# The last four tiles' output projection in another order, the last tile finished in quarters, and new durations for the planner: an attention and mixture kernel on one core

## The chip, the core and the metric

One NeuronCore of a Trainium2 chip runs the whole kernel. Its engines work side by side: TensorE (PE in the profile; PEld is its weight load), VectorE (DVE), ScalarE (ACT), GpSimd (POOL), and the queue SP, which issues the DMAs. The metric is the time of one execution on the device, in microseconds (us).

## What is computed

The input is four sequences of 512 tokens with 1024 features, in float32.

```python
x = x + layernorm(attention(layernorm(x)))   # 32 heads of 32, 8 key/value heads, rotary, causal
x = x + layernorm(ffn(layernorm(x)))
# ffn(x): the logits of 8 experts; the two largest, by softmax, weigh the experts' low-rank products
result = x @ base_w.T + base_b
low = einsum('bsd,erd->ebsr', x, lora_A)                        # rank 16
result += 2.0 * einsum('ebsr,eor,bse->bso', low, lora_B, w_full)
```

Each layernorm has no learned factors: it subtracts the mean and divides by the root of the variance and 1e-5.

## The kernel before

**Tiles.** The 2048 tokens are 16 tiles of 128. They are worked through in the order 0 to 11, 13, 14, 15, 12, in pairs (`pairs`, L834): the last two pairs are (13, 14) and (15, 12). Tile 12 is the first of its sequence and so attends to 128 keys alone; tile 15 attends to 512.

**Stages of a tile.** x is normalised (`normed_x`, L871) and transposed (pt_xn); keys and values come from a weight that stays on chip (acc_kv); q comes from streamed weights (acc_q), is rotated on DVE and POOL (`rotate`, L744) and transposed (pt_q; pt_k for keys). Scores (sc, `scores`, L1364) go to PSUM; DVE adds the mask and takes the maximum (nmax, L1451), ACT the exponentials (pr, L1393), POOL multiplies by the inverse sum (L1407), PE transposes (pt_p, L1467), ACT or DVE copies (prT), and PE multiplies by the values (av, L1490), which are copied to aT. The output projection o (acc_o) goes with its bias to the tile w; two layernorms follow (`attended`, L1050): w normalised is added to y, which holds x, and y normalised goes back to w. w is transposed (pt_h) and copied (T_h); the gates and the low-rank product (acc_gl, pt_low) and the base weight f (acc_f, with one matmul of the lora weight in each sum) follow, and a last layernorm, whose result is added to y and written out (`finished`, L1246). All plain matmuls have one line, that of `project` (L602).

**Products of pairs.** For a pair of tiles q, o and f are each made by seven products of half size rather than eight (`seven`, L641), from sums of the tiles' halves (s_q, s_o, s_f) and of the weights' quarters ("mixed", written to DRAM at the start). The last pair (15, 12) goes tile by tile (`whole`, L620): two accumulations of eight matmuls of 512 columns, nine for f.

**What orders the work.** The instructions are recorded by a planner in the kernel itself (`Order`, L92). It holds a clock for PE and one for each other engine. Each operation is written with a duration in us and an urgency, and is issued on the engine that can begin it first; each PE step names what it needs. `tensor` (L236) takes the next PE step from several lanes: scores, transposes, values, and three lanes of plain matmuls: the gates' (gl), the keys' (kv), and the main one, with q, o and f in the order that the kernel's last lines write down. A lane whose first step is not ready by the planner's clock is passed over. So the durations do nothing on the chip: they decide only the order in which each engine's instructions stand. PE's own costs are among them: `TILING` (L32) is added for a step of small tiled matmuls (scores, values), `PAIRED` (L33) where a score step and a value step go together. `LANDS` (L376) is the time from a DMA's issue to its data.

**Weights.** Pieces of 128x512 (256 KB) come in the order of the main lane through a ring of 13 buffers (`bring_pieces`, L476), on SP's queue, which also loads x and y and writes the output.

**The end.** Before, the main lane ends with f of (13, 14), o of 15, o of 12, f of 15, f of 12. The last tile's `finished` takes statistics of each half (L511), the mean and variance (L519), the root on POOL (L527), the shift (L531), then w = w*rstd + shift for each half on DVE or ACT (L546, L552), y + w on POOL or DVE (L343), and the DMA of each half (L1264).

Of the kernel before, what the change touches and what calls it, by code (L numbers as in the profile page):

```python
# [11 lines left out]
F32 = mybir.dt.float32  # L12
AF = mybir.ActivationFunctionType
ALU = mybir.AluOpType
AX = mybir.AxisListType

P = 128
# [11 lines left out]

SIGNAL = 0.1  # L30
FILL = 0.3
TILING = 0.4  # L32
PAIRED = 0.55  # L33
TURNING = 0.05
SAFE = 0.3

# [229 lines left out]
def kernel(  # L266
# [72 lines left out]
    def combine(urgent, out, in0, in1, op, engines=("dve", "pool")):  # L339


        def issue(engine):
            engine.tensor_tensor(out=out(), in0=in0(), in1=in1(), op=op)  # L343

        on = {"dve": (0.68, partial(issue, nc.vector)), "pool": (1.3, partial(issue, nc.gpsimd))}
        return Op(urgent, **{e: on[e] for e in engines})


# [24 lines left out]
    wlora_sb = const.tile([P, D], F32, name="wlora_sb")  # L373
    bbase_sb = const.tile([P, D], F32, name="bbase_sb")

    LANDS = 2.0  # L376
    RATE = 370.0
    loaded = {}

# [115 lines left out]
    class Norm:  # L495


        def __init__(self, name, urgent):
            self.name, self.urgent = name, urgent
            self.stats = None  # L500

        def half(self, src, h):
# [11 lines left out]
        def scale(self):  # L514
            name = self.name

            def aggr():
                self.mv = small.tile([P, 2], F32, tag="mv", bufs=4, name=f"mv_{name}")
                nc.vector.bn_aggr(out=self.mv, in_=self.stats)  # L519

            def eps():
                self.veps = small.tile([P, 1], F32, tag="veps", bufs=4, name=f"veps_{name}")
                nc.vector.tensor_scalar_add(self.veps, self.mv[:, 1:2], EPS)  # L523

            def root():
                self.rstd = small.tile([P, 1], F32, tag="rstd", bufs=4, name=f"rstd_{name}")
                nc.gpsimd.tensor_tensor(out=self.rstd, in0=self.veps, in1=neg_half, op=ALU.pow)  # L527

            def shift():
                self.shift = small.tile([P, 1], F32, tag="shift", bufs=4, name=f"shift_{name}")  # L530
                nc.gpsimd.tensor_scalar(  # L531
                    self.shift, self.mv[:, 0:1], self.rstd, -1.0, ALU.mult, ALU.mult
                )

            yield dve(0.2, self.urgent, aggr)
            yield dve(0.15, self.urgent, eps)
            yield pool(0.6, 0, root)
            yield pool(0.4, 0, shift)

        def apply(self, dst, src, h):  # L540
            cols = slice(h * 512, (h + 1) * 512)
            yield Op(
                self.urgent,
                dve=(
                    0.7,
                    lambda: nc.vector.tensor_scalar(  # L546
                        dst()[:, cols], src()[:, cols], self.rstd, self.shift, ALU.mult, ALU.add
                    ),
                ),
                act=(  # L550
                    0.65,
                    lambda: nc.scalar.activation(  # L552
                        dst()[:, cols], src()[:, cols], AF.Identity, bias=self.shift, scale=self.rstd
                    ),
                ),
            )
# [35 lines left out]
    def project(lhsT, w, n, name, needs, take):  # L592


        acc = []
        steps = []

        def issue(c):
            if not acc:
                acc.append(ps.tile([P, 512], F32, tag="ps", name=f"acc_{name}"))  # L600
            last = c == len(needs) - 1
            nc.tensor.matmul(  # L602
                acc[0][:, :n], lhsT=lhsT(c), rhs=w(c), start=(c == 0), stop=last
            )
            if last:
                start(take(acc[0], steps_of[c].done), order.now)

        for c in range(len(needs)):
            us = 0.858 if n == 512 else 0.24
            steps.append(Step(us, partial(issue, c), needs[c], bank=(c == 0)))  # L610
        steps_of = list(steps)
        return steps
# [4 lines left out]
            start(piece.used(step.done))  # L617
        return steps

    def whole(name, tok_name, k, lhsT, ready, take, room, used=None, more=None):  # L620
# [6 lines left out]
        return with_pieces(  # L627
            used,
            project(
                lambda c: lhsT()[:, c, :] if c < ND else more[0](),  # L630
                lambda c: used[c].sb if c < ND else more[1],
                512,
                f"{name}_{tok_name}_{k}",
                needs,
                take,
            ),
        )
# [106 lines left out]
    def rotate(raw, n, i, name):  # L744

        nh, half = n // HD, HD // 2
        yield turn_slots.take()
        turn = ropes.tile([P, 512], F32, tag="turn", name=f"turn_{name}")
        raw3, turn3 = (a[:, :n].rearrange("p (h d) -> p h d", d=HD) for a in (raw, turn))
        for a, b in ((0, half), (half, 0)):  # L750
            sin = rope_sb[:, i, 1, a : a + half].unsqueeze(1).to_broadcast([P, nh, half])
            yield dve(
                0.1 + n * 0.00065,
                2,
                lambda: nc.vector.tensor_tensor(
                    out=turn3[:, :, a : a + half],
                    in0=raw3[:, :, b : b + half],
                    in1=sin,
                    op=ALU.mult,
                ),  # L760
            )
# [6 lines left out]
        yield dve(  # L768
            0.1 + n * 0.0012,
            2,  # L770
            lambda: nc.vector.tensor_add(raw[:, :n], raw[:, :n], turn[:, :n]),
        )
        turn_slots.give(order.at)
# [472 lines left out]
    def finished(tok):  # L1246

        t = tok.t
        norm = Norm(f"4_{t}", 3)
        halves = [Task() for _ in range(NH)]  # L1250
        added, out_halves = [Task() for _ in range(NH)], [Task() for _ in range(NH)]

        def ended(h):
            yield from norm.half(lambda: tok.w, h)
            halves[h].finish(order.at)

        def out_half(h):
            yield from norm.apply(lambda: tok.w, lambda: tok.w, h)
            yield from add_half(lambda: tok.y, lambda: tok.w, h, 2, tok.last)
            added[h].finish(order.at)  # L1260
            cols = slice(h * 512, (h + 1) * 512)
            yield sp(
                0.7,
                lambda: nc.sync.dma_start(  # L1264
                    out=out[t * P : (t + 1) * P, cols], in_=tok.y[:, cols]
                ),
            )
            yield LANDS
            out_halves[h].finish(order.at)

        def rest():
# [10 lines left out]
        return ended  # L1282

    def ffn(pair):

# [43 lines left out]
        def take(h, acc, done):  # L1329
# [34 lines left out]
    def scores(g):  # L1364
# [19 lines left out]
        def quadrant(r):  # L1384
# [264 lines left out]
    order.tensor(score_lane, turn_lanes, value_lane, [gl_lane, kv_lane, main_lane])  # L1649
# [77 lines left out]
```

## Time and profile before

| What | us |
|---|---|
| median of the runs (three, 1186.48 to 1186.75) | 1186.6 |
| the profiled execution's own time | 1187.5 |
| its span, from the first to the last instruction | 1185.7 |
| TensorE busy in it | 1145.5 |
| VectorE busy | 823.9 |
| GpSimd busy | 608.0 |
| ScalarE busy | 533.1 |
| share of the DMA engines' time that the hardware queue took | 59.0% |

The page of the profile gives each engine's busy time and cuts the span into 40 slices of 29.6 us; a digit is a slice's busy share in tenths. PEclk is the granted clock of TensorE, also in tenths. A row of the timeline has the start, the length, the engine, the line, the operation, what it writes and reads, and in brackets the idle time of its engine just before it with what ended that. An x at a row's end counts instructions; a float32 matmul of 512 columns is two of them, 0.43 us each.

### The profile page before, as it was taken

How to read it: one execution, taken by the hardware profiler on the slowest of the kernel's cores; microseconds unless marked ns; L12 is line 12 of the kernel's file. 1: busy time of each engine (PE TensorE's matmuls, PEld its weight loads, DVE VectorE, ACT ScalarE, POOL GpSimd, SP SyncE). 2: the span in 40 equal slices, each digit the busy share in tenths (PEclk: the TensorE clock that was granted, in tenths of full speed). 3: DMA queues.
4: the chain of work that ended last, by engine and by line, in shares of the span. 5: the costliest groups of instructions: out<-in, count | busy, mean ns of one | idle time of the engine just before them, and what ended most of it. 6: DMA issues, size and time to landing. Idle time of an engine off the chain costs nothing.

```text
span 1185.7 us, 21412 instructions
## 1 busy us (share of the span) xinstructions
PE 1145.5 (97%) x7248; PEld 627.0 (53%) x7248; DVE 823.9 (69%) x1609; ACT 533.1 (45%) x1555; POOL 608.0 (51%) x857
## 2 busy tenths in 40 slices
PE   7999999999999999999999999999999999998996
PEld 3445545555556555565545555556655555545443
DVE  4687877875778756787667775678866786675353
ACT  0355544555555345454524334456543554552010
POOL 2575866553656536456455444545544564544221
PEclk9999999999999999999999999999999999998998
DMA  9869768434672636635377344762457645573883
GB/s 347 292 233 350 248 216 264 152 124 152 218 253 74 195 119 226 206 108 174 120 244 244 126 160 143 226 210 81 161 179 244 214 134 164 168 267 110 284 303 110
DMA packets 118315, 232.52 MB, mean 196 GB/s; under 512 B 13504, under 2 KB 14528, under 8 KB 118208
## 3 DMA queue, kind: packets, MB, share of 16 engines
q1 hardware_dynamic: 118208, 231.16, 59.0%
q8 instruction: 58, 0.95, 0.3%
q14 instruction: 49, 0.40, 0.1%
HBM read 210.14 MB, written 20.97 MB: 195 GB/s over the span
## 4 chain that ended last, share of the span: by engine, by line
PE 80%; DVE 8%; DMA 4%; POOL 4%; ACT 2%; issue 1%; SPq 0%; POOLq 0%; ACTq 0%; DVEq 0%
PE acc_f L602 19%; PE acc_o L602 15%; PE acc_q L602 11%; PE pt_p L1467 11%; PE acc_kv L602 7%; PE sc L1372 6%; PE av L1490 6%; PE acc_gl L602 2%; DVE nmax L1451 2%; POOL pr L1407 2%; ACT pr L1393 1%; PE pt_h L577 1%; DVE sc L1441 1%; DMA mix_o<-in_w_o_dram 1%; PE pt_q L996 1%
## 5 line engine op out<-in xcount | busy, mean ns | idle before, releaser
L1407 POOL TENSOR_SCALAR pr<-pr,rtot 128x256 f32<-128x256 f32 (+3 forms) x512 | 303.9, 610 | 249.3 <-DVE rtot L1422 183.9
L1393 ACT ACTIVATE pr<-sc,nmax 128x256 f32<-128x256 f32 (+3 forms) x512 | 264.6, 537 | 108.7 <-DVE nmax L1451 60.8
L1451 DVE TENSOR_REDUCE nmax<-sc 128x2 f32<-128x768 f32 (+3 forms) x176 | 198.2, 1126 | 32.6 <-ACT pr L1393 28.7
L1467 PE MATMUL pt_p<-ident,pr 128*128 128x128 f32 x1280 | 174.2, 276 | 3.5 <-POOL pr L1407 1.6
L1467 PEld LDWEIGHTS pt_p<-ident,pr 128*128 128x128 f32 x1280 | 144.1, 141 | 61.4 <-issue 46.5
L335 ACT COPY prT<-pt_p 128x512 f32<-128x512 f32 (+1 forms) x264 | 135.2, 548 | 83.6 <-PE pt_p L1467 82.9
L1441 DVE TENSOR_TENSOR sc<-sc,cmask 128x256 f32<-128x256 f32 (+2 forms) x176 | 96.7, 549 | 41.0 <-PE sc L1372 35.0
L602 PE MATMUL acc_kv<-wkv_sb,T_xn 128*128 128x512 f32 x256 | 119.4, 600 | 0.0
L335 ACT COPY aT<-av 128x128 f32<-128x128 f32 (+2 forms) x82 | 25.6, 312 | 195.0 <-PE av L1490 195.0
L1393 ACT ACTIVATION_READ_ACCUMULATOR pr<-sc,nmax 128x1 f32 x512 | 108.9, 213 | 0.0
L602 PE MATMUL acc_f<-piece,T_h 128*128 128x512 f32 x232 | 108.7, 596 | 0.0
L602 PE MATMUL acc_o<-piece,aT 128*128 128x512 f32 x232 | 106.3, 595 | 0.5 <-DMA piece<-in_w_o_dram 0.3
L602 PE MATMUL acc_q<-piece,s_q 128*128 128x512 f32 x224 | 105.1, 597 | 1.2 <-DVE raw_q L713 0.9
L602 PE MATMUL acc_o<-piece,s_o 128*128 128x512 f32 x224 | 103.4, 593 | 0.7 <-PE av L1490 0.7
L602 PE MATMUL acc_f<-piece,s_f 128*128 128x512 f32 x224 | 103.6, 593 | 0.0
L602 PE MATMUL acc_q<-piece,T_xn 128*128 128x512 f32 x224 | 102.7, 594 | 0.0
L343 POOL TENSOR_TENSOR y<-y,w 128x512 f32<-128x512 f32 x62 | 80.1, 1307 | 29.5 <-ACT w L552 15.1
L1372 PE MATMUL sc<-kT,qT 32*128 32x384 f32 (+3 forms) x1024 | 93.9, 464 | 0.6 <-ACT pr L1393 0.6
L527 POOL TENSOR_TENSOR rstd<-veps,neg_half 128x1 f32<-128x1 f32 x64 | 35.2, 554 | 114.5 <-DVE veps L523 114.2
L1490 PEld LDWEIGHTS av<-prT,v 128*32 128x32 f32 x2560 | 64.5, 109 | 49.8 <-issue 39.3
L1490 PE MATMUL av<-prT,v 128*32 128x128 f32 x2560 | 88.1, 276 | 0.0
L336 DVE COPY prT<-pt_p 128x512 f32<-128x512 f32 (+1 forms) x88 | 56.2, 641 | 32.2 <-PE pt_p L1467 31.5
(151 smaller groups left out, 1406.5 us busy)
## 6 DMA issues: line engine op xcount, KB each, us to landing
piece<-in_w_o_dram SPq DMA_DIRECT2D x116, 256.0 KB, 3.8
piece<-in_w_base_dram SPq DMA_DIRECT2D x116, 256.0 KB, 3.3
piece<-mixed_q SPq DMA_DIRECT2D x112, 256.0 KB, 3.5
piece<-mixed_o SPq DMA_DIRECT2D x112, 256.0 KB, 4.3
piece<-mixed_f SPq DMA_DIRECT2D x112, 256.0 KB, 3.4
piece<-in_w_qkv_dram SPq DMA_DIRECT2D x100, 256.0 KB, 3.7
xa<-in_x_dram SPq DMA_DIRECT2D x32, 256.0 KB, 4.1
y<-in_x_dram SPq DMA_DIRECT2D x16, 512.0 KB, 5.3
```

Of the source, the lines that this page charges most:

```text
L335: act=(0.15 + n * 0.00085, lambda: nc.scalar.copy(out(), in_())),
L336: dve=(0.15 + n * 0.00105, lambda: nc.vector.tensor_copy(out(), in_())),
L343: engine.tensor_tensor(out=out(), in0=in0(), in1=in1(), op=op)
L527: nc.gpsimd.tensor_tensor(out=self.rstd, in0=self.veps, in1=neg_half, op=ALU.pow)
L602: nc.tensor.matmul(acc[0][:, :n], lhsT=lhsT(c), rhs=w(c), start=(c == 0), stop=last)
L1372: nc.tensor.matmul(sc[:, r, c * n : (c + 1) * n], lhsT=tok.qT[g.kt][rows, (g.at + c) % GROUP, :], rhs=seq.kT[g.kt][rows, :n], start=True, ...
L1393: lambda: nc.scalar.activation(pr[:, c * n : (c + 1) * n], sc4[:, r, c, :], AF.Exp, bias=nmax[:, r, c : c + 1], accum_out=total[:, r, c : ...
L1407: lambda: nc.gpsimd.tensor_scalar(pr[:, c * n : (c + 1) * n], pr[:, c * n : (c + 1) * n], rtot[:, r, c : c + 1], 1.0, ALU.mult, ALU.mult,),
L1441: lambda: nc.vector.tensor_tensor(out=diag, in0=diag, in1=cmask.unsqueeze(1).unsqueeze(1).to_broadcast([P, q, g.n, P]), op=ALU.add,),
L1451: lambda: nc.vector.tensor_reduce(nmax[:, some, : g.n], sc4[:, some], AX.X, ALU.max, negate=True),
L1467: nc.tensor.transpose(pt[:, j, :], g.pr[r][:, j * P : (j + 1) * P], ident)
L1490: nc.tensor.matmul(av[r * HD : (r + 1) * HD, c, :], lhsT=g.seq.v[j][:, head * HD : (head + 1) * HD], rhs=g.prT[r][:, c * (i + 1) + j, :], ...
```

## The change

It has four parts.

1. The durations that the planner works with are set to others: TILING and PAIRED are lower, the two-input operations on DVE, the layernorm's step on ACT, the rotation, the exponentials and LANDS are longer, the layernorm's step on DVE is shorter.
2. In the main lane, the first half of o of tile 15 now stands ahead of f of (13, 14), the second half behind it.
3. f of the last tile (12) is made in four accumulations of 256 columns; each weight piece is used by two of them, and sum, bias and statistics follow each.
4. The end of the last tile: as soon as the root is there, DVE computes y = w*rstd + y for each half, and ACT adds the shift, which POOL makes meanwhile.

```diff
-TILING = 0.4
-PAIRED = 0.55
+TILING = 0.3
+PAIRED = 0.46
...
-        on = {"dve": (0.68, partial(issue, nc.vector)), "pool": (1.3, partial(issue, nc.gpsimd))}
+        on = {"dve": (0.85, partial(issue, nc.vector)), "pool": (1.3, partial(issue, nc.gpsimd))}
...
-    LANDS = 2.0
+    LANDS = 2.8
...
+        def quarter(self, src, k):
...
+            yield dve(
+                0.4,
+                self.urgent,
+                lambda: nc.vector.bn_stats(out=self.stats[:, k, :], in_=src()[:, cols]),
+            )
...
             yield pool(0.6, 0, root)
+            if rooted:
+                rooted.finish(order.at)
             yield pool(0.4, 0, shift)
...
                 dve=(
-                    0.7,
+                    0.66,
...
                 act=(
-                    0.65,
+                    0.82,
...
-            us = 0.858 if n == 512 else 0.24
+            us = {512: 0.858, 256: 0.432}.get(n, 0.24)
...
-                0.1 + n * 0.00065,
+                0.1 + n * 0.00088,
...
-            0.1 + n * 0.0012,
+            0.1 + n * 0.0013,
...
         def out_half(h):
-            yield from norm.apply(lambda: tok.w, lambda: tok.w, h)
-            yield from add_half(lambda: tok.y, lambda: tok.w, h, 2, tok.last)
+            cols = slice(h * 512, (h + 1) * 512)
+            y = tok.y[:, cols]
+            if tok.last:
+                yield dve(
+                    0.75,
+                    0,
+                    lambda: nc.vector.scalar_tensor_tensor(
+                        y, tok.w[:, cols], norm.rstd, y, ALU.mult, ALU.add
+                    ),
+                )
+                yield shifted
+                yield act(
+                    0.65,
+                    0,
+                    lambda: nc.scalar.activation(y, y, AF.Identity, bias=norm.shift),
+                )
+            else:
+                yield from norm.apply(lambda: tok.w, lambda: tok.w, h)
+                yield from add_half(lambda: tok.y, lambda: tok.w, h, 2)
...
         def rest():
-            yield halves
-            yield from norm.scale()
+            yield quarters if tok.last else halves
+            start(scaled(), order.at)
+            yield rooted if tok.last else shifted
...
+        def take_quarter(k, acc, done):
+            yield done
+            cols = slice(k * 256, (k + 1) * 256)
+            yield dve(
+                0.42,
+                0,
+                lambda: nc.vector.tensor_add(tok.w[:, cols], acc[:, :256], bbase_sb[:, cols]),
+            )
+            banks.give(order.at)
+            yield from ended[0](k)
...
-                    0.42 + n * 0.00092,
+                    0.5 + n * 0.00079,
...
-                    0.3 + n * 0.00085,
+                    0.33 + n * 0.00089,
...
-    for n, pair in enumerate(pairs[:-1]):
+    for n, pair in enumerate(pairs[:-2]):
         out_of(pair)
         if n + 2 < len(pairs):
             q_of(pairs[n + 2])
         ffn_of(pair)
-    for tok in pairs[-1]:
-        out_of([tok])
+
+    out_of(pairs[-2])
+    late, behind = pairs[-1]
+    at = len(main_lane)
+    out_of([late])
+    first_half, second_half = main_lane[at : at + ND], main_lane[at + ND :]
+    del main_lane[at:]
+    main_lane.extend(first_half)
+    ffn_of(pairs[-2])
+    main_lane.extend(second_half)
+    out_of([behind])
     for tok in pairs[-1]:
         ffn_of([tok])
```

`ND` is 8, the number of matmuls of one half of o; `late` is tile 15 and `behind` tile 12.

More of the change, by code (lines that the diff above doesn't have):

```diff
@@ L500, in __init__ @@
             self.stats = None
+        def quarter(self, src, k):
+            if self.stats is None:
+                self.stats = small.tile(
+                    [P, 2 * NH, 6], F32, tag="stats4", bufs=1, name=f"stats_{self.name}"
+                )
[5 more added lines that the diff above has]
+            )
         def half(self, src, h):
@@ L512, in half, with scale @@
             )
-        def scale(self):
+        def scale(self, rooted=None):
             name = self.name
@@ L618, in with_pieces, with whole @@
         return steps
-    def whole(name, tok_name, k, lhsT, ready, take, room, used=None, more=None):
+    def whole(name, tok_name, k, lhsT, ready, take, room, used=None, more=None, cols=None):
         used = used or block(name, plain, 0, k) + block(name, plain, 1, k)
@@ L630, in whole @@
                 lambda c: lhsT()[:, c, :] if c < ND else more[0](),
-                lambda c: used[c].sb if c < ND else more[1],
-                512,
-                f"{name}_{tok_name}_{k}",
+                lambda c: (used[c].sb if c < ND else more[1])[:, cols or slice(0, 512)],
+                cols.stop - cols.start if cols else 512,
+                f"{name}_{tok_name}_{k}" + (f"_{cols.start}" if cols else ""),
                 needs,
@@ L1251, in finished @@
         added, out_halves = [Task() for _ in range(NH)], [Task() for _ in range(NH)]
+        quarters, rooted, shifted = [Task() for _ in range(2 * NH)], Task(), Task()
         def ended(h):
@@ L1255, in ended, with ended_quarter @@
             halves[h].finish(order.at)
+        def ended_quarter(k):
+            yield from norm.quarter(lambda: tok.w, k)
+            quarters[k].finish(order.at)
         def out_half(h):
-            yield from norm.apply(lambda: tok.w, lambda: tok.w, h)
-            yield from add_half(lambda: tok.y, lambda: tok.w, h, 2, tok.last)
+            cols = slice(h * 512, (h + 1) * 512)
[17 more added lines that the diff above has]
+                yield from add_half(lambda: tok.y, lambda: tok.w, h, 2)
             added[h].finish(order.at)
-            cols = slice(h * 512, (h + 1) * 512)
             yield sp(
@@ L1264, in out_half @@
                 lambda: nc.sync.dma_start(
-                    out=out[t * P : (t + 1) * P, cols], in_=tok.y[:, cols]
+                    out=out[t * P : (t + 1) * P, cols], in_=y
                 ),
@@ L1269, in out_half, with scaled @@
             out_halves[h].finish(order.at)
+        def scaled():
+            yield from norm.scale(rooted)
+            shifted.finish(order.at)
         def rest():
-            yield halves
-            yield from norm.scale()
+            yield quarters if tok.last else halves
+            start(scaled(), order.at)
+            yield rooted if tok.last else shifted
             for h in range(NH):
@@ L1281, in finished @@
         start(rest())
-        return ended
+        return ended_quarter if tok.last else ended
     def ffn(pair):
@@ L1336, in take @@
             yield from ended[0](h)
-        steps = []
+        def take_quarter(k, acc, done):
+            yield done
+            cols = slice(k * 256, (k + 1) * 256)
+            yield dve(
+                0.42,
+                0,
+                lambda: nc.vector.tensor_add(tok.w[:, cols], acc[:, :256], bbase_sb[:, cols]),
+            )
+            banks.give(order.at)
+            yield from ended[0](k)
+        steps = []
+        if tok.last:
+            for h in range(NH):
+                used = block("f", plain, 0, h, 2) + block("f", plain, 1, h, 2)
+                for q in range(2):
+                    steps += whole(
+                        "f",
+                        tok.t,
+                        h,
+                        tok.hT_tile,
+                        tok.h_ready,
+                        partial(take_quarter, 2 * h + q),
+                        [],
+                        used,
+                        (lowT(0), (lo, hi)[h], [tok.low_done, loaded["lora"]]),
+                        slice(q * 256, (q + 1) * 256),
+                    )
+            return steps
         for h in range(NH):
```

## The prediction

> **What bounds the kernel.** I read the page's busy times first, then its 40 slices, then the stretches around the two slices that are not full, then TensorE's waits.
>
> ```profile
> PE 1145.5 (97%) x7248; PEld 627.0 (53%) x7248; DVE 823.9 (69%) x1609; ACT 533.1 (45%) x1555; POOL 608.0 (51%) x857
> PE   7999999999999999999999999999999999998996
> PEclk9999999999999999999999999999999999998998
> ```
>
> TensorE (PE) is the bound. The change takes none of its work away, so a gain can only come from PE's idle time and from what follows its last matmul. The idle lies in the first slice, in slice 37 (where the granted clock dips too) and in the last. The stretches, with columns for length, busy time by engine, granted clock and DMA:
>
> ```profile
> 20.00:150.00 130.00, 123.06 (x750) 65.85 (x748) 97.06 (x167) 59.48 (x196) 85.25 (x115) 1.00 0.82 287
> ...
> 1064.70:1070.60 5.90, 0.01 (x1) 0.02 (x1) 3.92 (x13) 5.31 (x30) 3.07 (x8) 0.92 0.20 67
> 1070.60:1077.00 6.40, 6.36 (x24) 4.90 (x25) 3.33 (x7) 1.07 (x2) 6.30 (x14) 0.54 0.00 0
> 1077.00:1131.00 54.00, 53.40 (x186) 25.88 (x184) 24.05 (x58) 6.48 (x11) 15.35 (x20) 1.00 0.73 239
> ```
>
> PE does nothing for 5.90 us, and then works 6.4 us at a clock of 0.54. The timeline says what it waited for:
>
> ```profile
> 59.05 0.63 PE L996 MATMUL pt_q<-ident,raw_q 128*128 128x128 f32 x4 [1.51 <-DVE raw_q L771]
> 107.36 0.63 PE L996 MATMUL pt_q<-ident,raw_q 128*128 128x128 f32 x4 [1.27 <-DVE raw_q L771]
> 224.33 0.63 PE L996 MATMUL pt_q<-ident,raw_q 128*128 128x128 f32 x4 [1.28 <-DVE rank L1163]
> 1070.61 2.23 PE L577 MATMUL pt_h<-ident,w 128*128 128x128 f32 x8 [5.90 <-DVE rtot L1422]
> ```
>
> All idle rows of PE sum to 30.1 us: 7.0 at the start, 5.9 here, 1.2 in small waits after it, and **16.1 in some 25 small waits before 1064**. Of those, 8.4 are transposes of rotated q and k (pt_q, pt_k). The end, from the last matmul's results at 1176.54 to 1185.7, is 9.2:
>
> ```profile
> 1178.49 0.55 POOL L527 TENSOR_TENSOR rstd<-veps,neg_half 128x1 f32<-128x1 f32 x1 [12.79 <-DVE veps L523]
> 1179.14 0.27 POOL L531 TENSOR_SCALAR shift<-mv,rstd 128x1 f32<-128x1 f32 x1
> 1179.44 0.81 ACT L552 ACTIVATE w<-w,shift,rstd 128x512 f32<-128x512 f32 x1 [15.61 <-POOL shift L531]
> 1180.07 1.26 POOL L343 TENSOR_TENSOR y<-y,w 128x512 f32<-128x512 f32 x1 [0.67 <-DVE w L546]
> 1180.29 1.60 DVE L343 TENSOR_TENSOR y<-y,w 128x512 f32<-128x512 f32 x1 [0.30 <-ACT w L552]
> 1181.91 0.81 SPq L1264 DMA_DIRECT2D out_dram<-y  x2
> ```
>
> **Step 1: the first half of o for tile 15 moves into the gap.** I compared the orders of the built programs, which hold no time. In the changed one, eight acc_o matmuls of tile 15 stand between tile 15's last value product and pt_h of tile 13, where there was one of another product. Each is two passes of 0.43, so they fill 6.9 us. Only the last of them waits for the newest copy into aT; their weight pieces are the next of a ring of 13, and the DMA share of 0.20 and 0.00 in the gap shows that the queue had nothing left to do, so no transfer is late.
>
> The wait does not vanish, since VectorE's (DVE) chain gets later: the last product of tiles 13 and 14 now puts two matmuls ahead of the last scores (1.7 us), so on equal work the last maximum (L1451) ends at 1066.2 instead of 1064.4. Behind it on DVE stand four rows of 0.69 (an add, three statistics), 0.55 for w, two aggregates of 0.2, two of 0.15, a reciprocal of 0.2: 4.2 us, and 0.2 for GpSimd's (POOL) add; then two roots of 0.55 and two shifts of 0.27 on POOL, of which DVE waits out 0.9; then 1.0 for tile 14 and 0.55 for tile 13's half: 1073.0. PE ends the eight at 1071.3 (the values at 1064.4 and 6.9). A wait of 1.7 us remains.
>
> The clock: in the window 20 to 150 PE waited up to 1.51 us at a time at a granted clock of 1.00, so a wait of 1.7 should not lower it. From pt_h to the last group's pt_p, PE has 4.5 us of work and took 7.5 at the low clock. The same stretch after the change: pt_h from 1073.0 to 1073.9, T_h copied at 1074.6 (behind an add of 0.69), four gl matmuls (0.93), one f (0.86), four gl, two f: pt_p at 1079.0. Before, it began at 1078.1 with nine matmuls (7.7) less behind it. **Gain 6.9.** Bounds: 0 if the chain ends as much later as work was moved; 8.9 if both the idle 5.9 and the 3.0 at half clock go.
>
> The Trainium skill, "TensorE: Matmul & The Clock Gate", Part 1, says that the clock is halved after an idle window of about 3.4 us and comes back after one as long of work. The trace agrees: 5.90 us idle, then 0.54. By that rule the 1.7 us is harmless, and one twice as long would not be.
>
> **Step 2: the planner's durations.** They change every engine's order, on 73 to 74 score-value pairs and the same number of switches between tiled and plain matmuls, so PE's own work stays equal (the two sums of rows by duration differ by under 0.1). The four narrow last products take 36 rows of 256 columns for 18 of 512: at 0.116 for 136 columns and 0.43 for 512 the price follows the columns, so nothing. What changes is how much PE work stands between a chain's start and its transposes. For tile 0's second half of q (the 1.51) it was six matmuls, four pt_p and two pt_xn, 7.8 us; now 9.1. The others: 9.1 to 9.9 (wait 0.53), 7.3 to 8.2 (1.27), 8.7 to 15.2 (0.94), 17.8 to 28.6 (0.60), 12.6 to 17.8 (0.68), pt_k 4.2 to 7.8 (0.88) and 6.3 to 6.4 (0.70); one falls, 15.4 to 14.2 (1.28). Taking each wait less its added cover leaves 3.7 of 8.4. Against it: the first pt_p of tile 2 has 6.9 us of cover where the smallest that stood without a wait is 8.1 (1.2), and one value product of tile 1 follows its transposes at once, so it waits out a copy of 0.59 and the hand-over (0.9). **Gain 2.6.** The other 7.7 of small waits I leave as they are. Bounds: all 16.1 go; or as much again is lost as I expect to win.
>
> **Step 3: the end.** The last add and statistics are over 256 columns. The add has a row (v, 0.42 against 0.69); the statistics have none: between 0 and 0.69, and I take 0.37, by the add's ratio. Saved 0.6. Then DVE does w*rstd+y twice; no row has it at this size; I take 0.69, the two-input add alone (ends: 0.55 of w, 1.60 of the add beside POOL). It no longer waits for the shift, but starts beside it, and the add of 1.60 above, which ended 0.56 after POOL's, shows that it will first wait: 0.28. So after rstd: 0.09 + 0.28 + 0.69 + 0.69 = 1.75 for the second half, ScalarE's (ACT) add of the shift 0.81 (row L552), hand-overs: 2.76, when its DMA is issued. Before, the last DMA was issued 3.28 after rstd. Saved 0.5, and 0.1 since the two transfers lie apart. **Gain 1.2**, bounds 0.3 to 2.0.
>
> The Trainium skill, "SBUF — State Buffer", Who interferes with whom, says that a DVE instruction with two SBUF inputs and a reading GpSimd instruction exclude each other for a whole instruction. That speaks against step 3; without it the sum would be 0.3 better.
>
> The tile-12 pt_low is now followed at once by the matmul that needs its copy (0.41 wait, the row of tile 15 before), while tile 15's gets half a pt_h between: nothing in sum.
>
> **Sum.** 6.9 + 2.6 + 1.2 = 10.7. The profiled run took 1187.5 (span 1185.7 and 1.8 around it), 0.9 over the median shown: 1176.8 by its own time, **1175.9** by the median.
>
> **Rivals.**
> - Steps 1 and 3 pay, the new order elsewhere nothing, or costs 2: 1178.5 to 1180.5. For: the 7.7 of other waits are reshuffled blindly. Chance 0.22.
> - The small waits fall by 6 to 8: 1170.5 to 1172.5. For: seven of nine covers grew by 0.8 us or more. 0.15.
> - pt_h's chain ends later than worked out (each row of mine can meet POOL, as the 1.60 does), the wait grows to where the clock falls again. That lies between 1.51 us, which left it at 1.00, and 5.90, which did not; at the middle, 3.7, it is 2.0 more idle and 2.4 of slow clock: 1180.3. 0.08.
> - The change does nothing that can be measured (0.2% is about what can be told): 0.04.
> - **Slower.** Longer planned chains put plain matmuls earlier, and the last tiles' attention (960 to 1050) is left without filler: eight groups of tile 15 each waiting for pr. It turns the result from 13.1 us of such waits on (10.7 and 2.4), 1.6 per group: 1190 and above. Against: the cover of those groups is 9.7 to 11.9 us against 8.7 to 13.2 before, and 900 to 1050 is full today. 0.08.
>
> The forecast has 0.43, from 1173 to 1178. Eight in ten: 1170 to 1182. Faster 0.88, same 0.04, slower 0.08.
>
> **What would show it.** Step 1: the row pt_h near 1070 has an idle of 1 to 2.5 us and a granted clock of 1.00 follows. Step 2: the pt_q rows' idle sums to under half. Step 3: from the last matmul's result to the last DMA issue 4.7 us instead of 5.8. Wrong if the 0.54 clock is back, or PE idles over 3 us at a new place.

## The result, and the profile after

The changed kernel takes **1167.5 us** (median of five runs, 1167.1 to 1170.9) against 1186.6 (1185.2 to 1188.0): a ratio of 0.984, with a 95% interval of 0.9822 to 0.9858. It is 19 us faster, nearly twice the 10.7 forecast, and 2.5 below the range's end of 1170. The profiled execution took 1167.07 by its own time, with a span of 1165.3 (before: 1187.52 and 1185.7).

The busy times and the slices of the changed kernel, from its page:

```profile
PE 1139.3 (98%) x7284; PEld 632.8 (54%) x7284; DVE 829.1 (71%) x1635; ACT 529.2 (45%) x1543; POOL 601.5 (52%) x847
PE   7999999999999999999999999999999999999997
PEclk9999999999999999999999999999999999999999
```

Slice 37 is full and its clock is back. The 36 more instructions of PE are the narrow products. What TensorE (PE) still waits for (the dots stand for rows left out): the total, how often, and the longest of each:

```profile
PE pt_xn L593 <- DVE xa L562: 7.3, 1, 7.3
PE pt_q L1013 <- DVE rtot L1496: 1.8, 1, 1.8
PE pt_xn L593 <- DVE prT L336: 1.1, 1, 1.1
PE pt_p L1541 <- DVE raw_k L951: 1.1, 1, 1.1
PE pt_h L593 <- DVE w L562: 0.9, 1, 0.9
PE pt_p L1541 <- DVE prT L336: 0.7, 1, 0.7
...
PE pt_k L962 <- DVE raw_k L788: 0.5, 1, 0.5
```

The sum of PE's idle rows falls from 30.1 to 17.8. The small waits ahead of the gap, 16.0 before in 27 rows (16.1 in the prediction; 8.4 of them for pt_q and pt_k), are 8.4 now (1.8 and 0.5 for pt_q and pt_k).

The stretch of the gap, in PE's timeline:

```profile
1053.89 7.13 PE L618 MATMUL acc_o<-piece,aT 128*128 128x512 f32 x16
1061.97 1.06 PE L593 MATMUL pt_h<-ident,w 128*128 128x128 f32 x8 [0.94 <-DVE w L562]
1063.38 1.19 PE L618 MATMUL acc_gl<-wgl_sb,T_h 128*128 128x136 f32 x8 [0.35 <-DVE T_h L336]
```

and in windows around it (length, busy PE, PEld, DVE, ACT, POOL, granted clock, DMA share, GB/s):

```profile
1060.80:1062.00 1.20, 0.26 (x2) 0.07 (x2) 1.20 (x3) 0.49 (x1) 1.20 (x3) 1.00 0.90 258
1062.00:1068.00 6.00, 5.65 (x31) 3.93 (x32) 4.95 (x15) 0.30 (x1) 5.90 (x13) 1.00 0.46 152
```

The sixteen passes of o fill the place, the wait is 0.94 where it was 5.90, and the clock behind it is 1.00 where it was 0.54.

**Where the 19 us come from.** For each amount of PE work done, the two traces give the time at which PE began the next piece. The difference is the **lead** of the changed kernel. It is 1.9 at 63 us, 5.3 at 118, 6.9 at 174, 9.4 at 255, and stands at 7 to 12 until the gap, where it is 10.6. It is 17.9 behind the gap and 18.7 at the last matmul. So the new durations brought **10.6** (nine of it in the first 250 us), the gap **7.3**, and 0.8 came behind it. The end adds 1.6: from the last matmul's result to the end of the span 7.53, before 9.17.

These four add up to 20.3, where the two profiled executions differ by 20.4; the medians differ by 19.1. A lead comes from one execution of each kernel. Six runs (the changed kernel and five of those below) have one and the same order up to the gap, and their leads at 1040 are 10.6, 10.6, 10.5, 10.2, 9.0 and 8.0. So a difference of up to 2.6 in a lead can be the execution's alone.

### The profile page after: what moved, and what is told of

It is laid out like the page before. It is cut to its first block, busy times and chain, and to the rows that moved or that the text cites. A ratio compares the mean times of both kernels' runs of the same rounds, so it can differ in the third digit from the quotient of the medians.

```text
span 1165.3 us, 21509 instructions
## 1 busy us (share of the span) xinstructions
PE 1139.3 (98%) x7284; PEld 632.8 (54%) x7284; DVE 829.1 (71%) x1635; ACT 529.2 (45%) x1543; POOL 601.5 (52%) x847
## 4 chain that ended last, share of the span: by engine, by line
PE 90%; DVE 5%; ACT 2%; POOL 1%; issue 1%; DMA 1%; POOLq 0%; ACTq 0%; SPq 0%; DVEq 0%
PE acc_f L618 19%; PE acc_o L618 16%; PE acc_q L618 15%; PE pt_p L1541 12%; PE acc_kv L618 9%; PE sc L1446 7%; PE av L1564 6%; PE acc_gl L618 2%; PE pt_q L1013 1%; DVE nmax L1525 1%; PE pt_xn L593 1%; PE pt_h L593 1%; ACT pr L1467 1%; DMA xa<-in_x_dram 1%; DVE sc L1515 1%
## 5 line engine op out<-in xcount | busy, mean ns | idle before, releaser
L618 PE MATMUL acc_f<-piece,T_h 128*128 128x512 f32 (+1 forms) x264 | 108.7, 541 | 0.0
```

The costliest lines, as they stand in the source:

```text
L618: nc.tensor.matmul(acc[0][:, :n], lhsT=lhsT(c), rhs=w(c), start=(c == 0), stop=last)
```

## The experiments

The theory formed after the result (**A**): the 10.6 comes from planned durations that now agree with the trace. The planner holds a start for every PE step, so the plan's starts can be laid beside the trace's. Beside the trace of before, PE is 5.3 us behind its own plan at 80 us, 10.0 at 160 and 11.1 at 242; with the new durations it is never more than 2.4 behind up to 800. The rivals: **B**, the move of o and the end were undersized; **C**, any new set of durations draws a new order, and this was a lucky draw; **D**, the cheaper tiled steps pay; and, later, that more cover pays, however much (cover is the PE work that stands between a chain's start and the PE step that waits for the chain's end). Each run is compared with the kernel before on its own chip; its interval is 95%. 

### Parts alone and parts left out

The changed kernel with all durations as before (three of the lines of part 1 are shown; all of them are set back):

```diff
-TILING = 0.3
+TILING = 0.4
...
-        on = {"dve": (0.85, partial(issue, nc.vector)), "pool": (1.3, partial(issue, nc.gpsimd))}
+        on = {"dve": (0.68, partial(issue, nc.vector)), "pool": (1.3, partial(issue, nc.gpsimd))}
...
-    LANDS = 2.8
+    LANDS = 2.0
```

> The changed kernel with all the planner's old durations; o of tile 15 moved, the quarters and the new end kept. Up to 1040 us its order is that of the kernel before. Theory A (the durations alone make the gain ahead of 1050 us, by giving chains more cover; the lead there was 10.6 us): only the gap at pt_h of tile 13 and the end are won, 7.3 + 1.7, so 1177.6. Theory B (the moved o and the end set off more than I counted, and the durations bring the 2.6 forecast): 1170.

Measured: 1176.2, ratio 0.991 (0.9894 to 0.9925). The lead is 1.1 at 1037 and 10.3 behind the gap.

The kernel before with all the new durations (the same lines the other way round):

> The kernel before with all the new durations and nothing else. Up to 1040 us its order is that of the changed kernel. Theory A: lead of 10.6 us at 1050, the idle of about 5 us at pt_h of tile 13 and the half clock stay (cover 12.8 us against 11.9), the end stays: 1176. Theory B: 1184.

Measured: 1177.7, ratio 0.9915 (0.99 to 0.9929). The lead is 10.6 ahead of the gap and 9.7 behind it. The two runs' gains, 10.2 and 8.7 us, add up to 18.9. The gain ahead of the gap is that of the durations, the rest that of the move and the end. By the times of whole executions the durations bring 8 to 10 us (8.7 by the medians; 2.6 forecast), a little less than the 10.6 of the two traces, and the move and the end 9 to 11 (10.2 by the medians; 8.1 forecast). So B holds for a small part of the miss, 1 to 3 us, and falls for the rest.

The changed kernel without the move of o:

```diff
-    for n, pair in enumerate(pairs[:-2]):
+    for n, pair in enumerate(pairs[:-1]):
...
-    main_lane.extend(first_half)
-    ffn_of(pairs[-2])
-    main_lane.extend(second_half)
-    out_of([behind])
+    for tok in pairs[-1]:
+        out_of([tok])
```

> The changed kernel without its part 2: both halves of o of tile 15 stand behind f of (13, 14) again. Step 1 of the prediction (6.9): 1174.4, with an idle of 5 to 6 ahead of pt_h of tile 13 and a granted clock of about 0.5 behind it. By the leads of the runs with one part (old durations: 9.2 gained there; new durations alone: 0.9 lost there): 1175.5 to 1176.7. If the new durations alone would have filled the gap: 1167.5 to 1169.

Measured: 1175.3, ratio 0.9912 (0.9891 to 0.9933). PE's timeline and two windows there:

```profile
1062.34 1.94 PE L593 MATMUL pt_h<-ident,w 128*128 128x128 f32 x8 [7.99 <-DVE rtot L1496]
```

```profile
1055.00:1061.00 6.00, 0.00 (x0) 0.00 (x0) 4.88 (x12) 4.96 (x28) 3.00 (x6) 0.80 0.07 22
1061.00:1067.00 6.00, 4.66 (x21) 3.88 (x22) 4.24 (x10) 0.67 (x1) 5.92 (x11) 0.63 0.00 0
```

With all the new durations the wait would have been 7.99, not 5.90 (with one row of them alone, below, it is 5.8: the orders ahead of it differ). With the move 0.94 of it is left.

### One row of the durations at a time

The kernel before with the rotation's two durations (0.00065 to 0.00088 and 0.0012 to 0.0013 for each column), and the kernel before with TILING 0.3 and PAIRED 0.46:

> The kernel before with the rotation's two durations alone (0.00088 and 0.0013 per column). If the rotated transposes are what waits, as the idle rows of the kernel before say (8.4 of 16.1 us), this alone brings most of the 10.6: the covers of pt_q of tile 2 go from 7.3 to 13.4 us, of tile 3 from 8.7 to 19.9; but those of tile 0's second half stay at 7.8 and 9.1. Theory A with rotation as the cause: 1179 to 1181. If it takes the accuracy of all durations together: within 2 us of 1186.6. Rival C (any other order moves the time by some us either way, by chance): no forecast, also slower.

> The kernel before with TILING 0.3 and PAIRED 0.46 alone. The order shows covers that shrink: pt_q of tile 2 from 7.3 to 5.6 and from 11.0 to 6.9 us, pt_k of tile 4 from 13.0 to 4.3, while pt_q of tile 0 gains 0.4. Theory A (covers decide): 2 to 5 us slower than before, 1188 to 1191, with longer waits at these transposes. Rival D (lower costs of the tiled steps are the part of the durations that pays): 1180 or less.

Measured: 1185.8, ratio 0.9989 (0.9979 to 0.9999), and 1185.9, ratio 0.9996 (0.9985 to 1.0006). Neither does it by itself; D falls. Theory A's own forecast for the second, 1188 to 1191, did not come either. At 242 us they are 10.5 and 8.8 behind their plans.

The kernel before with DVE's two-input operations alone (the first line below), the changed kernel with that row alone set back (the second), and the changed kernel with the old durations but for that row:

```diff
-        on = {"dve": (0.68, partial(issue, nc.vector)), "pool": (1.3, partial(issue, nc.gpsimd))}
+        on = {"dve": (0.85, partial(issue, nc.vector)), "pool": (1.3, partial(issue, nc.gpsimd))}
...
-        on = {"dve": (0.85, partial(issue, nc.vector)), "pool": (1.3, partial(issue, nc.gpsimd))}
+        on = {"dve": (0.68, partial(issue, nc.vector)), "pool": (1.3, partial(issue, nc.gpsimd))}
```

> The kernel before, with one duration changed: the two-input operations on DVE planned at 0.85 instead of 0.68. If this row alone carries the middle's gain: a lead of 6 to 10 at 1040 and a time of 1177 to 1181. If the gain needs the rows together (the rotation alone and the tiled costs alone brought 0 to 1.5): a lead of 0 to 4, and 1183 to 1187.

> The changed kernel, with one planned duration set back: the two-input operations on DVE at 0.68 instead of 0.85. If this one row carries the middle's gain: the lead at 1040 falls from 10 to under 4, 1173 to 1177. If the gain needs all the rows together, a third to a half of it goes: 1170 to 1173. If it is one of the others alone (the landing time, the layernorm's step and the exponentials), nothing: 1166.5 to 1168.5.

> The changed kernel with the old durations but for one: the two-input operations on DVE stay at 0.85 (their traced mean is 0.87 over 85 of them before and 0.85 over 94 after). If this row is the cause of the middle's gain: a lead of 7 to 10 at 1040, and 1166 to 1170. If its run in the kernel before was a lucky draw: a lead of 0 to 5, and 1171 to 1176.

Measured: alone in the kernel before 1176.2, ratio 0.9913 (0.989 to 0.9936), with a lead of 8.4 at 1040; set back in the changed kernel 1173.1, ratio 0.9874 (0.986 to 0.9889), lead 6.6; alone in the changed kernel **1167.0, ratio 0.9836 (0.9821 to 0.9851)**, lead 10.3. So this one row gives all that the six groups together give, and it pays in each of the three surroundings in which it was changed: 10.3, 8.8 and 4.0 us by the ratios. The others together, without it, give 6.6 of the 10.6 by the leads (4.3 by the ratios); the gains of single rows don't add. Alone, the row does not win in the same place: its lead is about 5 at 255 us, where all the groups had 9.4, then 7.8 at 400 and 10.0 at 900, and its trace is 4.3 behind its plan at 242. The groups of this line on DVE in the trace of before say what is special about it (busy us, mean ns of one; then idle before):

```profile
L343 DVE TENSOR_TENSOR raw_q<-raw_q,raw_q 128x512 f32<-128x512 f32 x12 | 10.9, 908 | 0.4
L343 DVE TENSOR_TENSOR w<-w 128x512 f32<-128x512 f32 x10 | 10.2, 1021 | 0.3
L343 DVE TENSOR_TENSOR w<-w,w 128x512 f32<-128x512 f32 x13 | 9.8, 757 | 0.4
```

and, for one of them, shortest, median and longest in ns:

```profile
L343 DVE TENSOR_TENSOR w<-w,w x13: 672/692/1554, 178.5 to 1103.7; 128x512 f32<-128x512 f32 x13
```

The median, 0.69 over all 85 of them, is close to the planned 0.68; the mean is 0.87, since 22 took over 0.9 and some 1.6 to 1.75. The plan had the median, and the order paid the mean. The trace shows where the long rows come from: each of the 22 began while a POOL instruction ran and ended 0.54 or 0.55 after that one's end, as the two adds at 1180 do in the prediction's rows (1.26 and 1.60). The 24 that began while POOL ran nothing took 0.67 to 0.69. The Trainium skill, "SBUF — State Buffer", Who interferes with whom, states the rule: a DVE instruction with two SBUF inputs and a reading GpSimd instruction exclude each other. The trace agrees with it.

### Right durations, long durations, or luck

All planned durations of DVE, ACT, POOL and SP in the changed kernel times 1.03, 0.97 and 1.3:

```diff
-        self.urgent, self.on = urgent, on
+        self.urgent, self.on = urgent, {e: (us * 1.03, f) for e, (us, f) in on.items()}
```

> The changed kernel, with every planned duration of DVE, ACT, POOL and SP times 1.03; only the order moves. Accuracy (the new durations follow the trace, so the order loses nothing against its plan): within 2.5 us of the 1167.5 of the changed kernel, that is 1165 to 1170, and the lead over the kernel before stays 8 to 12 us from 250 to 1040. Chance (any new set of durations draws another order, and this one was a lucky draw): a new draw, with a lead between 0 and 10 and a time of 1168 to 1178.

> The changed kernel, with every planned duration of the other engines times 0.97. Accuracy: 1165.5 to 1170.5, the loss against its own plan between 40 and 240 us under 3 us. Chance: another draw, 1168 to 1178, with no relation to the loss of the run at 1.03.

> The changed kernel, with every planned duration of the other engines times 1.3: far more PE work between the start of a chain and its transposes than the trace asks for. If cover is what pays, however much too long the durations are: 1163 to 1168, with the small waits nearly gone. If accuracy pays: too long is a loss as too short is, because plain matmuls are spent early as filler and other steps wait their turn though they are ready; 1172 or above, with waits at new places, late ones above all.

Measured: 1170.9, ratio 0.9856 (0.983 to 0.9882); 1174.3, ratio 0.9886 (0.9872 to 0.9901); 1290.5, ratio 1.0859 (1.0843 to 1.0875). The last one's slices:

```profile
PE   7969899996999889999799999999889988998997
PEclk9989899998999889999899999999879998898999
```

That cover pays however much it is, is refuted: at 1.3 PE is short of work in places all along. The plan itself has 174 us of idle PE there, and the trace 80 behind the first matmul. Accuracy's forecasts missed for the two small changes. At 0.97 PE is 9.7 behind its plan at 242 again (under 3 forecast), and the time is 7 us worse by the medians, 5 by the ratios. At 1.03 the time is 3 us worse by the medians, 2 by the ratios, just outside the forecast, and the lead is 3 at 250 where 8 to 12 was forecast. Both times lie in the range that was given for chance.

So the one row was varied by itself, at 0.76, 0.93 and 1.05:

> The changed kernel with that one row at 0.76, half way between the old 0.68 (1173.1) and the new 0.85 (1167.5). Accuracy: 1169 to 1172, and between 40 and 240 us the trace falls 3 to 6 behind the plan. Chance: anywhere from 1167 to 1176.

> The changed kernel with that one row at 0.93, as much above the traced mean as 0.76 is below. Accuracy: no more than 3 from 1167.5. More cover: 1165 to 1167. Chance: anywhere from 1167 to 1176.

> The changed kernel with the two-input operations on DVE planned at 1.05, above nine in ten... of the short form and 0.2 above the traced mean of 0.85. The curve so far: 0.68 1173.1, 0.76 1172.5, 0.85 1167.5, 0.93 1163.1. If too long a row costs as too short a one does: 1166 to 1171, back above 0.93. If this row pays the more cover it gives: 1160 to 1163.

| planned | 0.68 | 0.76 | 0.85 | 0.93 | 1.05 |
|---|---|---|---|---|---|
| median, us | 1173.1 | 1172.5 | 1167.5 | 1163.1 | 1179.2 |
| ratio | 0.9874 | 0.9880 | 0.9840 | 0.9803 | 0.9946 |
| 95% interval | 0.9860 to 0.9889 | 0.9866 to 0.9895 | 0.9822 to 0.9858 | 0.9787 to 0.9819 | 0.9931 to 0.9961 |

The time falls as the row comes up to its traced mean of 0.85 to 0.87, goes on falling a little above it, and rises by 16 us from 0.93 to 1.05. My "no more than 3 from 1167.5" at 0.93 missed by 1.4, on the good side, and the time lies below the other two ranges as well; 0.76 came out 0.5 above accuracy's range, and 1.05 far above both of its ranges. At 1.05, 7.6 us of lead are lost in one place, 112 to 149 us; the window there:

```profile
120.00:150.00 30.00, 24.56 (x186) 14.03 (x185) 22.43 (x40) 15.88 (x50) 25.40 (x28) 0.89 0.69 231
```

The runs at 0.97 and 1.03 lose there too (25.8 of 30 busy in each), and the changed kernel has its lowest share there (28.0 of 30, and 29.5 or more in each of the four windows of 30 around it).

The loss against the plan shows little of this. At 1.05 PE is 1.1 behind its plan at 118 and 3.2 at 160; it is the plan itself that leaves PE idle, 7.2 us between 112 and 150 (5.7 in the trace), against 2.0 in the plan of the changed kernel and none in that of the row alone. So a bad order shows in two ways: the trace falls behind a plan whose durations are too short, or the plan itself has PE wait, as it does where durations are too long.

What stays open: why 0.93 is better than the mean itself, and whether accuracy or the order that happens to be drawn makes the row at 0.85 pay. That it pays is shown three times; the reason is argued. A draw of 2 to 5 us shows in the runs at 1.03 and 0.97, and 4.4 is no more than that.

### The end

Without the quarters and without the new end; without the new end alone; and the changed kernel with another end, in which ACT and DVE subtract the mean from w while POOL takes the root, so that y = w*rstd + y ends it:

```diff
+                yield from norm.centre(lambda: tok.w, h)
+                yield rooted
                 yield dve(
                     0.75,
...
-                yield shifted
-                yield act(
-                    0.65,
-                    0,
-                    lambda: nc.scalar.activation(y, y, AF.Identity, bias=norm.shift),
-                )
```

> The changed kernel without its parts 3 and 4: f of the last tile in two sums of 512 columns, and the last tile's end as in the kernel before. The order up to the last tile's f is that of the changed kernel. Step 3 of the prediction (1.2): 1168.7. By the two profiles (9.3 from the last matmul's end to the end of the span before, 7.7 after): 1169.2, and the 9.3 is back. If the end had gained nothing, and the difference of the tails lay in the order ahead of it: 1167.5.

> The changed kernel without its part 4 alone: f of the last tile in four sums of 256 columns, but then the shift, w*rstd + shift and the add as in the kernel before. From the last matmul to the last statistics 0.6 less than in the kernel with 512 columns, and from the root to the last DMA's issue the 3.28 of before. Step 3 gave the quarters 0.6 of its 1.2: 1168.1; if they bring all of it (the new end of part 4 meets GpSimd's or DVE's other work): 1167.5; if part 4 brings nearly all: 1168.7 to 1169.2.

> The changed kernel with another end: while GpSimd takes the root, DVE and ACT subtract the mean from one half of w each, and after the root DVE does only y = w*rstd + y for each half; the shift on POOL and the add on ACT are gone. In the changed kernel the shift took 0.82 beside DVE's product where it takes 0.27 alone, and ACT's two adds of 0.67 stand behind it: from the root's end to the last DMA's issue 2.3. Here that is two products of 0.71 and a hand-over, 1.6, or 0.2 more where the subtraction ends after the root: the tail from the last matmul's result to the end of the span falls from 7.5 to 6.8 to 7.0, and the time to 1166.5 to 1167, under what the runs can tell. If the subtraction and the root exclude each other as the shift and the product did: 7.4 to 7.8.

Measured: 1167.7, ratio 0.9846 (0.9828 to 0.9864); 1167.8, ratio 0.9843 (0.9823 to 0.9862); 1167.0, ratio 0.9839 (0.9825 to 0.9854). The whole times can't tell these apart. The traces can, from the last matmul's result to the end of the span: before 9.17, without either 8.43, with the quarters 7.96, changed 7.53, centred 6.67. The first 0.7 is the planner's: without parts 3 and 4 it gives the first half's add to DVE,

```profile
1162.94 0.69 DVE L343 TENSOR_TENSOR y<-y,w 128x512 f32<-128x512 f32 x1
1163.25 1.50 POOL L343 TENSOR_TENSOR y<-y,w 128x512 f32<-128x512 f32 x1 [0.93 <-ACT w L568]
```

where in the kernel before POOL had it and DVE's own took 1.60. The changed kernel's end:

```profile
1159.29 0.55 POOL L541 TENSOR_TENSOR rstd<-veps,neg_half 128x1 f32<-128x1 f32 x1 [13.04 <-DVE veps L537]
1159.87 1.42 DVE L1288 SCALAR_TENSOR_TENSOR y<-w,rstd,y 128x512 f32<-128x512 f32 x2 [0.66 <-POOL rstd L541]
1159.93 0.82 POOL L545 TENSOR_SCALAR shift<-mv,rstd 128x1 f32<-128x1 f32 x1
1160.79 1.33 ACT L1296 ACTIVATE y<-y,shift 128x512 f32<-128x512 f32 x2 [16.42 <-POOL shift L545]
1161.54 0.96 SPq L1304 DMA_DIRECT2D out_dram<-y  x2
```

POOL's shift takes 0.82 beside DVE's product where it took 0.27 alone, and ACT waits for it. With the mean taken off during the root, both are gone:

```profile
1162.45 0.55 POOL L545 TENSOR_TENSOR rstd<-veps,neg_half 128x1 f32<-128x1 f32 x1 [13.05 <-DVE less L555]
1162.47 0.72 ACT L573 ACTIVATE w<-w,less 128x512 f32<-128x512 f32 x1 [14.94 <-DVE less L555]
1162.47 0.49 DVE L581 TENSOR_SCALAR w<-w,less 128x512 f32<-128x512 f32 x1
1163.08 1.41 DVE L1319 SCALAR_TENSOR_TENSOR y<-w,rstd,y 128x512 f32<-128x512 f32 x2
```

Last, that end together with the row at 0.93:

> The changed kernel with that row at 0.93 and with the end of the run before last, in which the mean is subtracted while the root is taken: the tail there was 6.6 from the last matmul's result to the end of the span, 7.5 in the changed kernel. The two are apart, so 1163.1 less 0.9: 1162.3. If the order at the end moves with the new end: 1162 to 1165.

Measured: 1163.3, ratio 0.9809 (0.9791 to 0.9826), the same as with the row at 0.93 alone (0.9803). So the 0.9 of the end does not show in the time. Both beat the kernel before and the changed one.

## Why the prediction was wrong, point by point

**What bounds the kernel**: right. PE's own work stayed equal, and the gain lies in its waits and at the end.

**Step 1, the gap**: right in mechanism and near in size. Forecast 6.9 (7.7 less the 0.9 between 1078.1 and 1079.0 is 6.8), a wait of 1.7 and no low clock; measured 7.3, a wait of 0.94 (and 0.35 for T_h), and a clock of 1.00. The last maximum ends at 1055.62, which is 1066.2 with the 10.6 of lead put back, as forecast. Without the move the changed kernel takes 7.8 us more (8.5 by the two ratios), and with the old durations the move brings 9.2 of lead: at 6.9 it was a little undersized. Of the signs it gave, the clock came, and the wait of 0.94 lies just under its 1 to 2.5.

**Step 2, the planner's durations**: this step failed. It had a gain of 2.6, and the runs show 10.6 by the two traces and 8 to 10 by the times. Its sign, pt_q's idle under half, came (6.8 to 1.8). The terms:
- "Taking each wait less its added cover leaves 3.7 of 8.4": 2.3 are left, 1.4 better, and not at the rows that were counted. The wait of 1.28 (tile 4), which was to grow to 2.5, is gone. Tile 2's pt_k has 0.52 where 0.6 was left to it. The other 1.78 is a new wait, of tile 3's second half of q, which had none before. That the sum came out near was luck.
- Two new waits, 1.2 in tile 2 and 0.9 in tile 1: of the first there is nothing, of the second 0.18. "The other 7.7 of small waits I leave as they are": with the two, that is 9.8 forecast, and 6.1 measured, among them 1.1 at a pt_p of tile 11 that nobody forecast. 3.7 better.
- The rest, 10.6 less the 7.6 by which the visible waits fell, is 3 that no idle row shows. Where in PE's rows it lies stays open.

The deeper fault is the method. I counted, chain by chain, the PE work ahead of the transposes, in an order in which every other engine's work had moved too. What could be read instead was there in the trace of before: PE falls 11 us behind its own plan in the first 242 us, and the trace contradicts a planned number by 0.19 in the mean of 85 rows, DVE's two-input operation, 0.68 against 0.87. (Others are contradicted as well, and less each: the exponentials and POOL's step behind them in 512 rows, the layernorm's step on ACT by 0.16 in 67.) That the 11 is near the gain is not a rule. By 1040 the kernel before is only 4.3 behind its plan; the row alone wins as much with its trace 4.3 behind at 242; at 1.05 it is 3.2 behind at 242, and the time is 12 us above the changed kernel's.

My bound, "all 16.1 go", held. My rival, that the small waits fall by 6 to 8, came: they fell by 7.6. The time came out 3 us below the range that I gave it, for the most part by what no idle row shows.

**Step 3, the end**: the mechanism was right, the size 1.2 against 1.6. From the last matmul's result to the last DMA's issue it is 4.35, where the forecast had 4.7. The quarters gave 0.5 (forecast 0.6). Part 4 gave 0.4 (forecast 0.5, and 0.1 for the transfers), but by other terms: DVE's product took 0.71 and waited for nothing, where I had 0.28 of waiting; it was POOL's shift that was held, 0.82 for 0.27. The remaining 0.7 came from the planner's durations, which moved an add to DVE; I had not looked for that. The exclusion that I weighed was there, but the other engine paid for it.

**The other rivals.** Low clock at pt_h: did not come. Slower through used-up filler: did not come with these durations (900 to 1050 is full). At 1.3 PE does run out of work, but all along and not only there.

## What to carry to other kernels

Where a kernel's order comes out of planned durations, compare the plan's own starts with the trace's, and look at the idle time in the plan itself: the stretch where the trace falls behind, or where the plan leaves the bounding engine idle, tells where the order is bad. How much there is to win, neither tells. Begin with the mean that an operation takes beside the others, not with its median or its time alone, and then vary it: here 0.93, a little over the mean, was the best of five values, 1.05 was worse than 0.68, and 1.3 times all durations was the worst of all. What two parts of a change gain in different stretches of the trace adds up (here 10.2 and 8.7); what two corrected durations gain in the same stretch does not.

## What was not expected of the hardware

The granted clock falls after shorter waits than the prediction allowed for, and not after each. In the run at 1.03 a wait of 1.76 from 86.4 us on was followed by this (windows from 88.1 on):

```profile
88.10:89.00 0.90, 0.86 (x2) 0.30 (x2) 0.00 (x0) 0.00 (x0) 0.90 (x3) 1.00 1.04 398
89.00:90.00 1.00, 1.00 (x9) 0.75 (x12) 0.70 (x2) 0.00 (x0) 0.65 (x2) 0.66 0.99 342
90.00:91.00 1.00, 1.00 (x12) 0.43 (x8) 0.33 (x1) 0.00 (x0) 0.00 (x0) 0.50 0.90 287
```

and in the run at 0.97 a wait of 2.63 left 0.50 for 6.8 us, while one of 2.30 in the same run left the clock at 1.00:

```profile
83.00:85.30 2.30, 0.04 (x1) 0.00 (x0) 2.30 (x5) 1.51 (x6) 1.30 (x2) 1.00 0.23 64
85.30:87.00 1.70, 1.66 (x6) 0.95 (x7) 1.70 (x5) 1.64 (x8) 1.49 (x3) 1.00 0.90 288
...
142.40:145.00 2.60, 1.66 (x8) 0.52 (x8) 2.60 (x4) 0.01 (x1) 2.60 (x3) 0.50 0.40 162
145.00:147.00 2.00, 1.54 (x6) 1.14 (x7) 1.97 (x3) 0.48 (x1) 2.00 (x4) 0.50 0.42 133
```

One wait even did both. Ahead of a pt_q at 134 us the changed kernel waits 1.78, and the run without parts 3 and 4, with the same order there, 1.77. The window behind it, first in the changed kernel, then in the other run:

```profile
134.00:137.00 3.00, 3.00 (x19) 1.58 (x18) 2.80 (x6) 1.27 (x5) 3.00 (x4) 1.00 0.50 194
134.00:137.00 3.00, 3.00 (x7) 1.44 (x6) 1.92 (x4) 1.16 (x3) 2.77 (x4) 0.50 0.57 222
```

It cost the second about 1.5 us of lead: one of the ways in which executions of one order come to differ.

What decides is where the wait lies. In each trace in which the clock changes more than once, the changes stand a whole number of 3.41 us apart, and all stretches of low clock but the last of a trace are 3.41 us long or a multiple of it. I divided all traces into stretches on this grid, from 28 us on, and took those that began at full clock. After each of the 22 in which PE was idle for 1.93 us or more, the clock was halved in the next; after none in which it was idle for 1.57 or less; of the 14 between, after 8. So PE idle for about half of one such stretch is enough, and a wait that a border divides does less: the 2.30 above lies as 1.30 and 1.00 in two of them.

So "a wait of 1.7 should not lower it" was not safe; that the clock stayed is shown only for this order, where the wait is 0.94. The Trainium skill, "TensorE: Matmul & The Clock Gate", Part 1, gives an idle window of about 3.4 us that runs free of the kernel. The traces agree with its length and with the free run. They don't agree that the whole window must be idle, by which the 1.7 would have been harmless; the measurement decides. What tips the cases between 1.61 and 1.89 stays open here.
